# Layer 2 of a four-layer graph network: exponentials formed as [column, row], with sums from a column of ones

## Chip, cores and metric

The kernel runs on one core of one Trainium2 chip. The metric is device time in microseconds (us) of one execution. The kernel before takes 1063.96 us, the median of three runs (1063.92 to 1064.11).

## What is computed

Four graph layers are applied in turn to x, 32 batches of 512 nodes with 128 features, all float32, over one adjacency matrix of 512 x 512. Each layer normalizes x per node, clips it at zero, runs its graph part and adds the result to x. Layer 2, the one that the change is named for, is a graph attention:

```python
def _L2_gnn_ref(h, adj, W, a, bias):
    Wh = jnp.einsum('bnf,fo->bno', h, W)
    f1 = Wh @ a[:F_out, 0]
    f2 = Wh @ a[F_out:, 0]
    e = jax.nn.leaky_relu(f1[:, :, None] + f2[:, None, :], negative_slope=0.2)
    e = jnp.where(adj[None, :, :] > 0, e, -9e15)
    attention = jax.nn.softmax(e, axis=2)
    h_prime = jnp.einsum('bij,bjo->bio', attention, Wh) + bias
    return jax.nn.elu(h_prime)
...
h = jnp.maximum(_layernorm(x, axis=-1), 0.0)
x = x + _L2_gnn_ref(h, adj, L2_gnn_W, L2_gnn_a, L2_gnn_bias)
```

Layer 0 is an attention whose scores pair neighbouring nodes; layer 1 is an attention weighted by the adjacency, followed by a normalization, an aggregation over neighbours and a small two-layer network; layer 3 multiplies by one fixed attention matrix that doesn't depend on x.

## The kernel before, in words

**Tiles.** A batch is a tile of 128 partitions x 4 chunks x 128 features (C = 4 chunks of nodes, 512 elements a partition). x of all batches stays on chip in xs. A score matrix of 512 x 512 is handled as four tiles y of 128 x 512.

**Engines.** TensorE (PE) does the products, all in float32, and the transposes, as products with an identity; a float32 product of 128 x 128 stands in the trace as two passes, a transpose as one. VectorE (DVE) and ScalarE (ACT) work on the results, GpSimd (POOL) on tiles outside PSUM, SyncE loads and stores. PSUM is used as 8 tiles ("banks") of 128 x 512.

**Layer 2 before.** preln gives the normalized, transposed hT (four transposes, line 419). project_scored (line 593) multiplies hT by w2_ext of 130 columns, so that h holds the 128 features and the two scores f1 (column P) and f2 (column P + 1). attend then works with rows of the score matrix on the partitions: four transposes repeat f2 over the partitions (prow, line 419); for each of four row blocks a fused DVE operation adds the mask and takes the row's maximum (line 620); two small operations make the negative maximum nmax (lines 631 and 635); ACT applies the leaky slope (line 645) and the exponential with its row sum (line 653), both in place in y; four transposes turn each y so that columns lie on the partitions (pt, line 419); the turned block is copied out of PSUM (line 412's helper for DVE, line 410's for ACT, two blocks each; in layer 1 it is multiplied by the adjacency on DVE instead, line 662); and sixteen products with h give po (line 673). Line 950 inverts the sums, line 953 applies them, POOL adds the bias (line 954), ACT and DVE form the elu (lines 958 and 959), and POOL adds it to xs (line 960).

**Other lines that the change touches.** In layer 0, DVE forms hs and hs2, h scaled by two factors per node (lines 803 and 804); ACT rounds hs2 (line 817), POOL forms the remainder (line 818), and products use both (lines 835 and 840). In layer 1, DVE takes mean and variance of zn (lines 509 and 511), and POOL raises the variance to the power -1/2 (lines 521 and 523). Before the layers, prepare and prepare_last make masks and weights: bias (0 or NEG by the adjacency) by rows, biasT by columns for the first 256 rows.

**The order of the work.** No loop sets it. Every operation is recorded with an engine, an assumed length, what it reads and writes, and for some a port count; Plan.run then places them by its own clock, engine by engine, taking the operation that can begin first and, among those within SLACK of it, the one with the earliest turn. A turn is the start of the chain (one layer of one batch; starts are GAPS apart, a layer LAGS batches behind layer 0) plus STRETCH times the way within it. The preparation has turns of its own (PREPARED, FILLED). The port count makes the plan keep marked DVE and POOL operations apart in time. A tile's buffer comes from a room of fixed size (8 banks, 8 for scores, 6 for h). Where the plan sees PE idle for over PAUSE it puts in transposes that compute nothing (line 332, "idle"). The result is a fixed order on each engine's queue; a queue runs strictly in that order, and an instruction whose inputs are late holds up all behind it.

Of the kernel before, what the change touches and what calls it, by code (L numbers as in the profile page):

```python
# [28 lines left out]
F32 = mybir.dt.float32  # L29
# [8 lines left out]
P = 128  # L38
NEG = -9.0e15
# [18 lines left out]
SLACK = 0.05  # L58

STRETCH = 3.7  # L60

PREPARED, FILLED = (27.0, 1.0), (135.0, 1.3)

RAMP = 3.7
# [3 lines left out]
GAPS, LAGS = (5.3, 12.0, 6.7, 5.4), (0, 6, 12, 16)  # L68
# [41 lines left out]
class Plan:  # L110
# [45 lines left out]
    def run(self):  # L156
# [17 lines left out]
        for _ in range(len(self.ops)):  # L174
# [35 lines left out]
            if op.engine is PE and begin - idle[PE] > PAUSE:  # L210
                wanted = sum(s.tile is None and s.room is self.banks for s in op.slots)
                if sum(free <= idle[PE] for free in self.banks.free) > wanted:
                    self.idle_products(begin - idle[PE])
# [42 lines left out]
def kernel(  # L256
# [40 lines left out]
    sm = ctx.enter_context(tc.tile_pool(name="sm", bufs=8))  # L297

# [7 lines left out]
    def small(name, shape=(P, C)):  # L306
        return sm.tile(list(shape), F32, name=name, tag=name)
# [65 lines left out]
    biasT = const("biasT", (P, C, N2))  # L373
# [26 lines left out]
    v_offT, v_adiag, v_adiag_rep = Value(), Value(), Value()  # L400
# [50 lines left out]
    for ib in range(C):  # L451
# [6 lines left out]
            wide(e.t).bitcast(BF16)[:, 0:N], bias[:, ib, :], 0.0, None, ALU.is_gt), [v_adj[ib]], [e])  # L458
# [24 lines left out]
    def mask_first():  # L483
        for jb in range(C):
            nc.vector.tensor_scalar(biasT[:, jb, :], adjT[:, jb, 0:N2], 0.0, NEG, ALU.is_le, ALU.mult)

    op(DVE, 0.8, mask_first, v_adjT[0:H], [v_biasT])
# [7 lines left out]
    op(DVE, 0.8, mask_second, [*v_adjT[H:], v_cnt], [v_mask2T])  # L495
# [20 lines left out]
    def inv_dev(mv):  # L516
        rstd = Value()

        def emit():
            ve = small("ve")  # L520
            nc.gpsimd.tensor_scalar(ve, mv.own[:, :, 1], LN_EPS, 1.0, ALU.add, ALU.mult)
            rstd.own = small("rstd")
            nc.gpsimd.tensor_tensor(rstd.own, ve, mhalf, ALU.pow)  # L523

        op(POOL, 1.3, emit, [mv], [rstd])
        return rstd
# [81 lines left out]
    def attend(h, src, v_src, v_h, weights, v_weights):  # L608
# [32 lines left out]
        for ib in range(C):  # L641
# [18 lines left out]
            if weights is not None:  # L660
                pT = value(turned, "pT")
                op(DVE, 0.6, lambda ib=ib, pt=pt, pT=pT: nc.vector.tensor_mul(pT.t, pt.t, weights[:, :, blk(ib)]),  # L662
                   [pt, *v_weights], [pT])
            elif ib < H:
                pT = value(by_act, "pT")
                copy_op(ACT, 0.49, lambda pT=pT: pT.t, lambda pt=pt: pt.t, [pt], [pT])
            else:
                pT = value(turned, "pT")
                copy_op(DVE, 0.6, lambda pT=pT: pT.t, lambda pt=pt: pt.t, [pt], [pT])
# [15 lines left out]
    def layer0(b):  # L685
        hT, _ = preln(b, POOL)
# [30 lines left out]
        for hf in range(H):  # L717

            def emit_max(hf=hf):
# [3 lines left out]
                for k in range(2):  # L723
                    jb = 2 * hf + k
                    nc.vector.tensor_tensor_reduce(
                        wide(y[hf].t)[:, k * N2 : k * N2 + N2], node[:, hf, :], biasT[:, jb, :], 1.0, LOWEST,
# [75 lines left out]
        dve(0.08, emit_rs2, [rs, e2], [rs2], port=1)  # L802
        op(DVE, 0.6, lambda: nc.vector.tensor_mul(hs.t, h[0].t[:, :, 0:P], per_chunk(rs.own)), [rs, *h], [hs], port=1)
        op(DVE, 0.6, lambda: nc.vector.tensor_mul(hs2.t, h[0].t[:, :, 0:P], per_chunk(rs2.own)), [rs2, *h], [hs2], port=1)
# [54 lines left out]
    def layer1(b):  # L859
# [61 lines left out]
        rz = inv_dev(variances(lambda c: zn.t[:, c, :], [zn]))  # L921
# [17 lines left out]

    def layer2(b):  # L940
        hT, _ = preln(b, POOL)
        h = project_scored(hT, w2_ext, [v_w2])
        po, ssum = attend(h, lambda: h[0].t[:, :, P], h, h, None, None)
        v1 = value(by_dve, "v1")

        rs = Value()

        def emit_rs():
            rs.own = small("rs")
            nc.vector.reciprocal(rs.own, ssum[0].own)  # L950

        dve(0.1, emit_rs, ssum, [rs])
        dve(0.6, lambda: nc.vector.tensor_mul(v1.t, po[0].t, per_chunk(rs.own)), [*po, rs], [v1])  # L953
# [39 lines left out]
    def prepare():  # L993
# [24 lines left out]
        for ib in range(C):  # L1018
            dve(0.31, lambda ib=ib: nc.vector.tensor_scalar(
                bias[:, ib, :], bias[:, ib, :], 0.0, NEG, ALU.is_le, ALU.mult), [], [v_adj[ib], v_bias])  # L1020
# [5 lines left out]
        def centred(dst, src, reads, writes):  # L1026
            def emit():
                s = small("row_sum", (P, 1))
                nc.vector.tensor_reduce(s, src(), AX.X, ALU.add)
                nc.vector.tensor_scalar(s, s, 1.0 / P, None, ALU.mult)  # L1030
                nc.vector.tensor_scalar(dst(), src(), s, None, ALU.subtract)

            dve(0.5, emit, reads, writes)
# [26 lines left out]
        dve(0.35, eye, [v_eps], [eye_e])  # L1060
        for jb in range(C):
            op(POOL, 0.6, lambda jb=jb: nc.gpsimd.tensor_copy(adjTe[:, jb, :], adjT[:, jb, :]), v_adjT, [v_adjTe], port=1)
            dve(0.2, lambda jb=jb: nc.vector.tensor_add(
                adjTe[:, jb, blk(jb)], adjTe[:, jb, blk(jb)], eye_e.t[:, 0, :]), [eye_e], [v_adjTe])
# [4 lines left out]
    def prepare_last():  # L1069
# [34 lines left out]
        for kb in range(C):  # L1104
            dve(0.31, lambda kb=kb: nc.vector.tensor_scalar(
                maskT_t(kb), adjT[:, kb, :], 0.0, None, ALU.is_gt), v_adjT, [maskT[kb]])
# [37 lines left out]
        dve(0.4, emit_before, [v_n], [v_before])  # L1144
# [12 lines left out]
        dve(0.4, emit_lo, [pb, v_n], [v_lo])  # L1157
# [18 lines left out]
        for ib in range(C):  # L1176
# [9 lines left out]
            dve(0.78, emit_in, [rank_k, v_lo], [ge_lo, in_row[ib]])  # L1186
# [9 lines left out]
        dve(0.3, emit_terms, [v_e], [v_terms])  # L1196
# [53 lines left out]
        for ib in range(C):  # L1250
# [45 lines left out]
            dve(0.31, emit_last, [v_e, v_lo, num[ib]], [share[ib]])  # L1296
# [5 lines left out]
            dve(0.72, emit_diag, [], [share[ib], dg, v_diag[ib]])  # L1302
# [56 lines left out]
```

## Time and profile before

| what | value |
|---|---|
| median of the runs shown | 1063.96 us |
| the profiled execution's own time | 1063.48 us |
| its span, first to last instruction | 1061.6 us |
| TensorE clock granted | 1.000 |
| idle transposes (line 332) | 158, busy 21.7 us |
| line 673, products of attention and h in layers 1 and 2 | 2048 passes, busy 242.2 us |
| line 419, transposes of y, layers 1 and 2 | 1024, busy 130.9 us |
| line 653, exponentials of layers 1 and 2 | 256, 714 ns each, and 256 reads of the sum, 191 ns each |
| line 412, turned blocks copied by DVE | 64, 684 ns each |
| line 410, turned blocks copied by ACT | 64, 587 ns each |

A "busy" time counts the time in which at least one instruction of the group ran; consecutive instructions overlap, so the distance between their starts is shorter than one's duration. A table by stretches of the span gives, for each engine, the busy time in the stretch and the number of instructions that began in it. The table of waits names the instruction that waited, what released it, the total wait, how often, and the longest.

### The profile page before, as it was taken

The page shows a single profiled execution, that of the slowest core. Times are in us where ns is not written, and L with a number is a line of the kernel's source. Part 1 is how long each engine was busy: PE and PEld are TensorE (multiplying, and loading weights), DVE is VectorE, ACT ScalarE, POOL GpSimd, SP SyncE. Part 2 cuts the span into 40 slices and gives each one's busy share as a digit, 9 for nine tenths or more (in the row PEclk, how much of TensorE's full clock was granted, in tenths as well). Part 3 has the DMA queues.
Part 4 walks back from the last instruction along what each step waited for, and adds up shares of the span by engine and source line. Part 5 has one row for each costly group of instructions (what it writes and reads, how often), then busy time and mean ns, then how long its engine had stood idle before and what let it go on. Part 6 is the DMA issues. An engine that isn't in the chain of part 4 may idle for free.

```text
span 1061.6 us, 25176 instructions
## 1 busy us (share of the span) xinstructions
PE 1043.7 (98%) x8483; PEld 964.5 (91%) x8483; DVE 875.3 (82%) x3698; ACT 766.2 (72%) x1984; POOL 795.8 (75%) x1176
## 2 busy tenths in 40 slices
PE   8999999999999999999999999999999999999998
PEld 7888888989998999999999999999899999999997
DVE  6999999989988878888888888888888877766752
ACT  3667888789777777777877777787777777767751
POOL 6999657779787768787778778777877666576772
PEclk9999999999999999999999999999999999999999
DMA  5500000000010000000000000000000000000001
GB/s 152 126 1 12 1 12 12 2 12 12 1 32 2 21 21 22 21 21 11 2 12 11 11 12 12 11 2 12 11 12 11 12 11 11 11 22 11 21 24 37
DMA packets 56911, 20.48 MB, mean 19 GB/s; under 512 B 21584, under 2 KB 56272, under 8 KB 56784
## 3 DMA queue, kind: packets, MB, share of 16 engines
q1 hardware_dynamic: 56784, 18.90, 7.2%
q8 instruction: 67, 1.10, 0.4%
q14 instruction: 60, 0.49, 0.2%
HBM read 10.43 MB, written 8.39 MB: 18 GB/s over the span
## 4 chain that ended last, share of the span: by engine, by line
PE 86%; DVE 8%; POOL 2%; ACT 2%; issue 1%; SPq 1%; DMA 0%; DVEq 0%; POOLq 0%; ACTq 0%
PE po L673 20%; PE pt L419 16%; PE po L982 10%; PE pg L909 10%; PE proj L593 7%; PE po L835 4%; PE prow L419 3%; PE p L579 3%; PE po L978 3%; PE px L579 3%; PE pz L579 2%; PE po L840 2%; DVE st L509 1%; PE po L845 1%; PE po L832 1%
## 5 line engine op out<-in xcount | busy, mean ns | idle before, releaser
L673 PE MATMUL po<-h,pT 128*128 128x128 f32 x2048 | 242.2, 275 | 0.1
L673 PEld LDWEIGHTS po<-h,pT 128*128 128x128 f32 x2048 | 236.1, 192 | 4.7 <-issue 3.3
L558 POOL TENSOR_SCALAR xn<-xs,shift,rstd 128x128 f32<-128x128 f32 x512 | 229.3, 462 | 2.4 <-DVE top L631 0.9
L653 ACT ACTIVATE y<-y,nmax 128x512 f32<-128x512 f32 x256 | 181.7, 714 | 5.4 <-DVE nmax L635 3.9
L523 POOL TENSOR_TENSOR rstd<-ve,mhalf 128x4 f32<-128x4 f32 x160 | 171.9, 1075 | 13.3
L620 DVE CUSTOM_DVE_ANT_0 y<-prow,bias 128x512 f32<-128x512 f32 x256 | 162.5, 683 | 1.9 <-PE prow L419 1.9
L982 PE MATMUL po<-h,offT 128*128 128x128 f32 x1024 | 135.4, 275 | 0.0
L419 PE MATMUL pt<-ident,y 128*128 128x128 f32 x1024 | 130.9, 274 | 0.5 <-ACT y L653 0.3
L909 PE MATMUL pg<-adjTe,hg 128*128 128x512 f32 x256 | 130.8, 593 | 0.0
L419 PEld LDWEIGHTS pt<-ident,y 128*128 128x128 f32 x1024 | 114.9, 141 | 13.0 <-issue 7.7
L982 PEld LDWEIGHTS po<-h,offT 128*128 128x128 f32 x1024 | 124.6, 192 | 0.0
L509 DVE BATCH_NORM_STATS2 st<-xs 128x6 f32<-128x128 f32 x512 | 109.5, 274 | 7.1 <-POOL xs L960 4.5
L593 PEld LDWEIGHTS proj<-w_ext,hT 128*128 128x128 f32 x768 | 96.7, 191 | 19.1 <-issue 10.3
L593 PE MATMUL proj<-w_ext,hT 128*128 128x130 f32 x768 | 103.4, 276 | 0.7 <-ACT hT L568 0.5
L645 ACT ACTIVATE y<-y,src 128x512 f32<-128x512 f32 x128 | 84.6, 713 | 23.1 <-DVE rmax L620 23.0
L960 POOL TENSOR_TENSOR xs<-xs,em 128x512 f32<-128x512 f32 x32 | 42.0, 1313 | 77.1 <-DVE em L959 64.0
L954 POOL TENSOR_TENSOR v<-v,rows 128x512 f32<-128x512 f32 x32 | 40.9, 1279 | 72.6 <-DVE v L953 72.6
L645 ACT ACTIVATE y<-y,h 128x512 f32<-128x512 f32 x128 | 84.8, 714 | 8.1 <-DVE rmax L620 7.7
L568 ACT ACTIVATE hT<-pt 128x512 f32<-128x512 f32 x128 | 73.7, 588 | 23.4 <-PE pt L419 11.7
L662 DVE TENSOR_TENSOR pT<-pt,adjT 128x512 f32<-128x512 f32 x128 | 82.5, 679 | 5.0 <-PE pt L419 4.9
L419 PE MATMUL pt<-ident,xn 128*128 128x128 f32 x512 | 80.1, 275 | 2.4 <-POOL xn L558 1.5
L410 ACT COPY h<-proj 128x260 f32<-128x260 f32 x192 | 66.1, 371 | 12.6 <-PE proj L593 11.2
(199 smaller groups left out, 2290.9 us busy)
## 6 DMA issues: line engine op xcount, KB each, us to landing
xs<-in_x_dram SPq DMA_DIRECT2D x32, 256.0 KB, 4.0
out_dram<-yo SPq DMA_DIRECT2D x32, 256.0 KB, 2.3
u<-h SPq DMA_DIRECT2D x128, 0.5 KB, 1.8
bias<-in_adj_dram SPq DMA_DIRECT2D x4, 256.0 KB, 3.8
wts<-in_L_gnn_W_dram SPq DMA_DIRECT2D x3, 64.0 KB, 3.0
rows<-in_L_gnn_bias_dram SPq DMA_DIRECT2D x2, 64.0 KB, 3.8
wt_o<-L_gnn_others_weight_dram SPq DMA_DIRECT2D x1, 64.0 KB, 2.4
wts<-n_L_gnn_self_weight_dram SPq DMA_DIRECT2D x1, 64.0 KB, 4.0
```

The lines of the kernel that those rows point to most:

```text
L419: nc.tensor.transpose(dst(k), src(k), ident)
L509: nc.vector.bn_stats(st[:, c, :], src(c))
L523: nc.gpsimd.tensor_tensor(rstd.own, ve, mhalf, ALU.pow)
L558: nc.gpsimd.tensor_scalar(xn.t[:, c, :], src[:, c, :], shift.own[:, c : c + 1], rstd.own[:, c : c + 1], ALU.add, ALU.mult,)
L579: nc.tensor.matmul(pt.t[:, c, :], lhsT=column(hT, c), rhs=w, start=True, stop=True)
L593: nc.tensor.matmul(p[:, c, :], lhsT=column(hT, 2 * k + c), rhs=w_ext, start=True, stop=True)
L620: nc.vector.tensor_tensor_reduce(wide(y[ib].t), wide(prow.t), bias[:, ib, :], 1.0, LOWEST, ALU.add, ALU.max, rmax.own[:, ib : ib + 1],)
L645: nc.scalar.activation(yw, yw, AF.Prelu, alpha=0.2, bias=src()[:, ib : ib + 1])
L653: nc.scalar.activation(yw, yw, AF.Exp, bias=nmax.own[:, ib : ib + 1], accum_out=ssum[0].own[:, ib : ib + 1])
L673: nc.tensor.matmul(po[ib].t[:, ib, :], lhsT=pT.t[:, jb, :], rhs=h[0].t[:, jb, 0:P], start=(jb == 0), stop=(jb == C - 1),)
L909: nc.tensor.matmul(wide(pg.t), lhsT=hg.t[:, nb, :], rhs=adjTe[:, nb, :], start=(nb == 0), stop=(nb == C - 1))
L982: nc.tensor.matmul(po[ib].t[:, ib, :], lhsT=offT[:, jb, blk(ib)], rhs=h1.t[:, jb, :], start=False, stop=(jb == C - 1),)
```

## The change

Layer 2 no longer calls attend. The row maxima are found as before, with the added scores written to a tile junk that nothing reads. The scores are then formed with columns on the partitions: f1 is repeated by four transposes (p_src), nmax by four more (p_max, copied to r_max by ACT); for each of four column blocks DVE adds p_src, the column's f2 and the mask biasT, ACT applies the leaky slope, POOL (two blocks) or DVE (two blocks) adds r_max, ACT takes the exponential. The result is used by PE as it is. The score column of h is overwritten with ones by POOL, so that products of 129 columns give the row sums as column 128; they now need two banks. biasT grows to all 512 rows and becomes bfloat16, and NEG becomes a power of two.

Besides, hs2 of layer 0 is formed by ACT; layer 1's second variance comes from four squares with sums on ACT; four centred weights are formed by ACT; adjTe is copied by ACT instead of POOL; some small tiles get 14 buffers instead of 8; and the plan's constants and several port counts and lengths change.

```diff
-NEG = -9.0e15
+NEG = -(2.0**53)
-SLACK = 0.05
-STRETCH = 3.7
-PREPARED, FILLED = (27.0, 1.0), (135.0, 1.3)
-RAMP = 3.7
+SLACK = 0.10
+STRETCH = 3.3
+PREPARED, FILLED = (33.0, 1.0), (152.0, 1.7)
+RAMP = 2.9
-GAPS, LAGS = (5.3, 12.0, 6.7, 5.4), (0, 6, 12, 16)
+GAPS, LAGS = (5.1, 11.7, 6.5, 5.2), (0, 5, 11, 15)
...
-    biasT = const("biasT", (P, C, N2))
+    biasT = const("biasT", (P, C, N), BF16)
...
+    def squares(src, reads):
+        sq = Value()
+        def emit():
+            sq.own = small("sq")
+            for c in range(C):
+                nc.scalar.activation(sq_out, src(c), AF.Square, accum_out=sq.own[:, c : c + 1])
+        op(ACT, 1.55, emit, reads, [sq])
+        return sq
...
+        def emit_hs2():
+            for c in range(C):
+                nc.scalar.mul(hs2.t[:, c, :], h[0].t[:, c, 0:P], rs2.own[:, c : c + 1])
-        op(DVE, 0.6, lambda: nc.vector.tensor_mul(hs2.t, h[0].t[:, :, 0:P], per_chunk(rs2.own)), [rs2, *h], [hs2], port=1)
+        op(ACT, 1.17, emit_hs2, [rs2, *h], [hs2])
...
-        rz = inv_dev(variances(lambda c: zn.t[:, c, :], [zn]))
+        rz = inv_dev(squares(lambda c: zn.t[:, c, :], [zn]), lambda sq: sq.own, 1.0 / P)
...
     def layer2(b):
-        po, ssum = attend(h, lambda: h[0].t[:, :, P], h, h, None, None)
+        prow = repeated(lambda k: h[0].t[:, k, P + 1 : P2], h)
+        junk = parts(scores, "junk", C)
...
+            op(DVE, 0.61, emit_top, [prow, v_bias], [junk[ib], top[ib]])
...
+        p_src = repeated(lambda k: h[0].t[:, k, P : P + 1], h)
+        p_max = repeated(lambda k: nmax.own[:, k : k + 1], [nmax])
+        r_max = value(by_act, "r_max")
+        copy_op(ACT, 0.49, lambda: wide(r_max.t), lambda: wide(p_max.t), [p_max], [r_max])
+        y = [value(scores, "y") for _ in range(C)]
+        for jb in range(C):
+            op(DVE, 0.61, lambda jb=jb: nc.vector.scalar_tensor_tensor(
+                wide(y[jb].t), wide(p_src.t), h[0].t[:, jb, P + 1 : P2], biasT[:, jb, :], ALU.add, ALU.add),
+               [p_src, v_biasT, v_biasT2, *h], [y[jb]])
+            op(ACT, 0.61, lambda jb=jb: nc.scalar.activation(wide(y[jb].t), wide(y[jb].t), AF.Prelu, alpha=0.2), [], [y[jb]])
+            engine, length, on = ((POOL, 1.25, nc.gpsimd), (DVE, 0.6, nc.vector))[jb % 2]
+            op(engine, length, lambda jb=jb, on=on: on.tensor_add(
+                wide(y[jb].t), wide(y[jb].t), wide(r_max.t)), [r_max], [y[jb]], port=1)
+            op(ACT, 0.61, lambda jb=jb: nc.scalar.activation(wide(y[jb].t), wide(y[jb].t), AF.Exp), [], [y[jb]])
+        ones = Value(h[0].slot)
+        op(POOL, 0.15, lambda: nc.gpsimd.memset(h[0].t[:, :, P : P + 1], 1.0), [neg, p_src], [*h, ones])
...
+                    nc.tensor.matmul(
+                        sums(ib // 2)[:, ib % 2, 0 : P + 1], lhsT=y[jb].t[:, ib, :], rhs=h[0].t[:, jb, 0 : P + 1],
+                        start=(jb == 0), stop=(jb == C - 1),
+                    )
+            op(PE, 0.9, emit_po, [*y, ones], [po[ib // 2]])
...
+                nc.vector.reciprocal(rs[0].own[:, 2 * k : 2 * k + 2], sums(k)[:, :, P])
+            dve(0.1, emit_rs, [po[k], *rs[0:k]], [rs[k]])
+            dve(0.35, lambda k=k: nc.vector.tensor_mul(
+                v1.t[:, 2 * k : 2 * k + 2, :], sums(k)[:, :, 0:P],
...
-            op(POOL, 0.6, lambda jb=jb: nc.gpsimd.tensor_copy(adjTe[:, jb, :], adjT[:, jb, :]), v_adjT, [v_adjTe], port=1)
+            op(ACT, 0.59, lambda jb=jb: nc.scalar.copy(adjTe[:, jb, :], adjT[:, jb, :]), v_adjT, [v_adjTe])
```

## The prediction

> **What bounds the kernel now.** I read the page's busy shares first, then the chain that ended last, then the table by stretches, and last the PE timeline of one batch. The page:
>
> ```profile
> span 1061.6 us, 25176 instructions
> ...
> PE 1043.7 (98%) x8483; PEld 964.5 (91%) x8483; DVE 875.3 (82%) x3698; ACT 766.2 (72%) x1984; POOL 795.8 (75%) x1176
> ...
> PE 86%; DVE 8%; POOL 2%; ACT 2%; issue 1%; SPq 1%; DMA 0%; DVEq 0%; POOLq 0%; ACTq 0%
> ```
>
> PE is busy nearly all the span and is 86% of the chain. A busy share can hide a slow start, so the stretches decide (columns: length, then busy time of PE, its weight loads, DVE, ACT and POOL with the number of instructions, granted clock, DMA share, GB/s):
>
> ```profile
> 25.00:50.00 25.00, 23.46 (x187) 20.49 (x186) 24.07 (x148) 15.28 (x53) 23.99 (x42) 1.00 0.54 131
> ...
> 75.00:100.00 25.00, 22.37 (x181) 20.44 (x180) 24.05 (x97) 17.67 (x50) 23.89 (x35) 1.00 0.07 13
> ...
> 200.00:300.00 100.00, 100.00 (x808) 91.89 (x807) 93.20 (x407) 84.01 (x226) 79.95 (x117) 1.00 0.03 7
> ...
> 400.00:500.00 100.00, 100.00 (x823) 93.05 (x822) 85.12 (x379) 74.72 (x199) 79.18 (x117) 1.00 0.08 18
> 500.00:600.00 100.00, 100.00 (x823) 93.01 (x823) 82.29 (x353) 72.90 (x190) 79.22 (x118) 1.00 0.05 12
> 600.00:700.00 100.00, 99.95 (x827) 93.27 (x826) 83.31 (x350) 73.80 (x196) 75.86 (x112) 1.00 0.04 10
> 700.00:800.00 100.00, 100.00 (x830) 93.49 (x829) 85.94 (x347) 76.82 (x193) 77.68 (x114) 1.00 0.04 10
> ```
>
> From 150 us on PE doesn't stop, at full clock. From 25 to 100 us DVE and POOL are both 96% busy and PE falls behind: the start is theirs. From 200 to 300 us DVE at 93% and ACT at 84% still leave PE full. These two rows are my scale for how much the other engines can bear.
>
> The timeline of PE gives the rate (start, length, instruction, number):
>
> ```profile
> 501.15 1.91 PE L419 MATMUL pt<-ident,y 128*128 128x128 f32 x16
> 502.90 0.60 PE L419 MATMUL pt<-ident,zn 128*128 128x128 f32 x4
> ...
> 510.49 0.60 PE L419 MATMUL prow<-ident,h 128*128 128x128 f32 x4
> 510.92 1.06 PE L579 MATMUL px<-wts,zT 128*128 128x128 f32 x8
> ...
> 532.29 1.91 PE L419 MATMUL pt<-ident,y 128*128 128x128 f32 x16
> ```
>
> Sixteen transposes of y take 502.90 - 501.15 = 1.75 us from start to start, four repeats of a row 0.43: 0.109 us each, both kinds alike. The same group returns after 532.29 - 501.15 = 31.14 us, the period of a batch with all four layers.
>
> **PE's part of the change.** Per batch 16 transposes of y go (line 419 as called from attend), and 8 come, for p_src and p_max: 8 x 0.109 = 0.87 us less, 27.9 us over 32 batches. The 32 passes of po stay, with 129 columns for 128. Eight passes of 130 columns take 0.90 us from start to start (line 593 at 523.40), eight of 128 take 0.89 (line 673 at 518.50): 0 to 0.04 us a batch, 0 to 1.3 in all; I take 0.6. Nothing hides these terms where PE is full, and layer 2 begins only after some 200 us. The listing of the changed program's PE queue holds 167 idle transposes for 158: 35 fewer in the start, 44 more later. 9 x 0.109 is +1.0 us. The new period is 31.14 - 0.87 = 30.27 us, if nothing else takes over.
>
> **DVE.** Added per batch: four score additions (nearest row: line 967, also a PSUM tile with an SBUF one, 0.58 from start to start; fused additions of line 620, 0.61) 4 x 0.61; two additions of r_max 2 x 0.61 (line 959, 0.61); one more reciprocal 0.08; the two halves of line 953 for one, 2 x 0.34 (line 853) - 0.61. Removed: two copies of pT 2 x 0.61, hs2 0.60, the variance of zn 1.06 (515.36 to 516.42). Net +0.93 us. A bfloat16 mask beside a float32 tile is in no row; 0.58 and 0.79 (line 1264, two scalars) bound each score addition, so the net lies between +0.8 and +1.7. The four stretches shown from 400 us average 84.2%, 26.2 us a batch; 27.1 of 30.27 is 90%.
>
> **ACT.** Added: four squares with sums, each 0.32 (line 925, busy over count) and a read of the sum 0.19, 2.04; hs2 4 x 0.32; r_max 0.56. Removed: two copies 1.12, four reads of sums 0.76. Net +2.0; down to +1.3 if the exponentials and slopes without a scalar operand run as line 904 does (630 ns for 714). 74.6% of 31.14 is 23.2 us; 25.2 of 30.27 is 83%, below the 84% seen beside a full PE.
>
> **POOL.** Added: two additions of 128x512, 1.28 each (lines 917 and 960), and the memset of ones, 0.10 to 0.25 (the constants' memsets, line 521). +2.7 us. 78.0% of 31.14 is 24.3 us; 27.0 of 30.27 is 89%. It is the largest growth, on a queue that now spends 6.9 us a batch waiting:
>
> ```profile
> POOL v L954 <- DVE v L953: 72.6, 24, 10.3
> POOL xs L960 <- DVE em L959: 64.0, 26, 6.9
> ```
>
> **The waits that are added.** PE's transposes of nmax wait for DVE. Behind them stand layer 0's products; ahead, between p_src and p_max, the changed queue has some 6 to 8 us of PE work in two neighbouring batches, against 4 x 0.61 + 0.2 = 2.6 us of DVE work. Between p_max and the products that need y lie about 100 passes, 11 us, against r_max 0.56, two POOL additions 2.6 and two exponentials 1.4, some 5 us with the handovers. So PE's margin is 3.5 to 6 us, which the queues of the others can use up. POOL's additions wait for ACT; behind them stand xn of other batches, and behind xn PE's next transposes. All four y now live until the last product, and junk takes a fifth buffer of 8. I price all this at +2 us, bounds 0 and +15.
>
> **The shared reads of DVE and POOL.** A row: POOL's addition of line 855 runs from 508.20 for 0.73 us, and DVE's ltn (line 752, two SBUF inputs of 4 elements) starts at 508.23 and takes 0.71, where its median is 0.216. It waited for POOL. Another: hs (line 803, two SBUF inputs) starts at 526.89 inside a rstd of POOL (526.13 to 527.15) and takes its usual 0.68; the power reads little and holds little. So the sum that must not overlap is POOL without five rstd, 27.0 - 5.1 = 21.9, and DVE's five large operations with two SBUF inputs, 3.05, and some 17 small ones at 0.1: 26.7 of 30.27 us, 88%. It fits.
>
> The Trainium skill, page "SBUF — State Buffer", section "Who interferes with whom", speaks against this change: a DVE instruction with two SBUF inputs and a GpSimd instruction that reads SBUF exclude each other for a whole instruction. Taken for rstd too, that would make 27.0 + 4.75 = 31.8 us a batch, more than 31.14, and a kernel slower by about 20 us; the row of hs inside rstd speaks for the smaller sum.
>
> **Start and end.** From 25 to 150 us the trace has 10 hs2 (6 us), four centred weights (line 1030 and its neighbours, some 3 us) and one variance on DVE that go to ACT, and 2.5 us of copies on POOL (line 1062) that do; 4 x 0.29 (line 485) come. DVE is relieved by some 9 us, POOL by less; I take -3 us, bounds -9 and +3. The last 60 us have PE waits of some 6 us in all, taken as they are.
>
> **Sum.** 1061.6 - 27.9 + 0.6 + 1.0 + 2 - 3 = 1034.3 us of span; outside it lie 1063.48 - 1061.6 = 1.9 us. That is 1036 us, against 1063.48 for the same execution; the median is 0.5 us above that. A difference of about 0.2%, 2 us, is the least that a measurement of this kernel can tell.
>
> **Rivals.**
> *A, PE stays the bound (0.62):* 1036, its own range 1026 to 1046.
> *B, the gain is half lost (0.17):* DVE at 90% or POOL at 89% holds PE up in stretches, as both do at 96% before 100 us, where PE gets 92%. For it: both now run above their mean of 400 to 800 us; against: the 93% of 200 to 300 us. Half of 27.9 gives 1050; 1046 to 1061.
> *C, POOL's waits stay (0.14), slower:* of the 6.9 us a batch that POOL waits at the head of its queue, those for v and em are dependences and not slack. If over 4.1 us stay (31.14 - 27.0), POOL's period passes the old one. With 4.9 kept it is 31.9, 0.8 x 32 = 25 us: 1088; with all of them 33.9, some 1150. Against it: the order of the queue was made anew, and a wait at the head shrinks when the queue fills.
> *D, no effect (0.03):* the end is set elsewhere than by PE's work, so 1064. The full rows speak against it.
> *E, the start shrinks too (0.04):* all of the 9 us that DVE loses there, and no new waits: 1020 to 1026.
>
> **Numbers.** Faster: A, B and E, 0.83; same 0.03; slower 0.14. The range 1020 to 1060 takes in E, A, nearly all of B, some 0.81; C and D stay out.
>
> **What would show it.** In the changed profile: 512 transposes of y for 1024 and 384 + 128 repeats for 256; the period of layers 0 to 3 near 30.3 us; PE still at 99 to 100 in the stretches from 200 to 800, with DVE near 90, ACT near 83 and POOL near 89. B would show as PE at 95 to 98 there, with waits of PE's weight loads on POOL's or ACT's y. C would show as PE at 90 and long waits of POOL's additions on ACT. I am wrong if the products of 129 columns over two banks run slower than 0.112 us a pass, or if an instruction on y takes over a fifth longer than its nearest row.

## The result, and the profile after

| | before | after |
|---|---|---|
| median of 4 runs | 1063.94 us (1063.11 to 1064.11) | 1075.97 us (1073.15 to 1077.79) |
| ratio | | 1.0113, 95% interval 1.01 to 1.0126 |
| profiled execution | 1063.48 us, span 1061.6 | 1077.17 us, span 1075.2 |

The change makes the kernel 12 us slower; 1036 us were forecast. The page of the changed kernel, in the same order as that of the kernel before (span; busy time, share and instructions of each engine; the chain that ended last):

```profile
span 1075.2 us, 24867 instructions
...
PE 1032.6 (96%) x8236; PEld 936.8 (87%) x8236; DVE 960.4 (89%) x3594; ACT 813.1 (76%) x2224; POOL 885.9 (82%) x1268
...
DVE 41%; PE 35%; POOL 11%; ACT 6%; issue 3%; SPq 2%; DMA 1%; DVEq 0%; POOLq 0%; ACTq 0%
```

PE has 11 us less to be busy with and the span is 13.6 us longer. The chain, which went through PE for 86% of its length, now goes through DVE for 41% and POOL for 11%. DVE has grown by 85 us, POOL by 90, ACT by 47. The stretches of the changed kernel (length, then PE, its weight loads, DVE, ACT, POOL, the granted clock, DMA share, GB/s):

```profile
200.00:300.00 100.00, 95.64 (x729) 83.63 (x728) 92.76 (x362) 89.99 (x255) 80.63 (x116) 1.00 0.03 7
...
400.00:500.00 100.00, 96.53 (x780) 87.90 (x779) 92.52 (x331) 78.35 (x214) 79.32 (x116) 1.00 0.07 17
500.00:600.00 100.00, 98.73 (x805) 90.72 (x804) 93.76 (x353) 78.30 (x215) 88.46 (x125) 1.00 0.06 12
600.00:700.00 100.00, 98.71 (x807) 91.02 (x806) 94.43 (x349) 77.25 (x217) 88.29 (x127) 1.00 0.05 12
700.00:800.00 100.00, 98.75 (x792) 89.73 (x791) 95.22 (x364) 80.06 (x221) 88.23 (x130) 1.00 0.04 10
```

PE is at 95.6 to 98.8% where it was full, and from 400 us on it starts 780 to 807 passes in 100 us where it started 823 to 830. A busy share hides short waits, since consecutive passes overlap. So I took from each trace the distances between the starts of consecutive passes: for each kind of pass, the distance at the lowest quarter is its work, and what goes beyond it by more than 15 ns is waiting. Summed over the span:

| us | work of PE | waits of PE | DVE busy | of it above the groups' medians | POOL busy |
|---|---|---|---|---|---|
| before | 1018.9 | 37.1 | 875.3 | 18.1 | 795.8 |
| after | 993.0 | 73.3 | 960.4 | 69.8 | 885.9 |

**PE's work fell by 25.9 us, as forecast (-26.3). Its waits grew by 36.2.** (The span grew by 3.3 us more than these two give; distances under the 15 ns and the two ends are not counted in them. Other ways of sorting the passes into kinds give 23 to 27 us for the first and 34 to 38 for the second.) They are spread: 0 to 200 us 21.6 (25.2 before), 200 to 400 us 16.0 (3.7), 400 to 800 us 16.6 (3.9), the rest 19.0 (4.3). The column "above the medians" is the part by which DVE's instructions last longer than the median of their own group, so it is time without added work. A group here is a line's instructions of one shape that also wait for and raise the same semaphores, and what is under some 50 ns isn't counted. With groups by line and shape alone the two numbers are 28 and 77: the growth is nearly the same, 49 us for 51.7.

The groups of DVE in the changed kernel that show it (busy us and mean ns of one, then the idle time before), and the one of ve in the kernel before:

```profile
L994 DVE SCALAR_TENSOR_TENSOR y<-prow,h,biasT 128x512 f32<-128x512 f32 x128 | 89.0, 743 | 0.0
...
L999 DVE TENSOR_TENSOR y<-y,r_max 128x512 f32<-128x512 f32 x64 | 62.7, 1003 | 4.7 <-ACT r_max L415 4.2
...
L897 DVE TENSOR_TENSOR ve<-q,mv 128x4 f32<-128x4 f32 x32 | 12.4, 387 | 0.0
```

```profile
L881 DVE TENSOR_TENSOR ve<-q,mv 128x4 f32<-128x4 f32 x32 | 5.1, 158 | 0.0
```

The score addition of line 994 takes 743 ns each time, 60 more than the fused additions. The additions of r_max (line 999) take 1003 ns in the mean; the table of that line gives the least, the median and the longest:

```profile
L999 DVE TENSOR_TENSOR y<-y,r_max x64: 656/692/3715, 195.3 to 1040.2; 128x512 f32<-128x512 f32 x64
```

The small ve, unchanged, took 158 ns in the mean (line 881 of before) and now takes 387, while its median went only from 154 to 158: some of the 32 wait long. What holds them is seen in one stretch. DVE's timeline of the changed kernel:

```profile
624.94 2.35 DVE L999 TENSOR_TENSOR y<-y,r_max 128x512 f32<-128x512 f32 x2
...
628.89 1.19 DVE L722 SCALAR_TENSOR_TENSOR ls<-sc 128x4 f32<-128x4 f32 x1
```

and POOL's in the same stretch:

```profile
624.87 1.28 POOL L1040 TENSOR_TENSOR xs<-xs,em 128x512 f32<-128x512 f32 x1 [2.02 <-DVE ve L897]
...
627.55 2.51 POOL L999 TENSOR_TENSOR y<-y,r_max 128x512 f32<-128x512 f32 x2
```

DVE's two additions start 0.07 us after POOL's addition and take 2.35 us; two of them take some 1.2 without it, so they wait till POOL ends at 626.15. The ls of four elements starts inside POOL's additions of y and ends at 630.08, when they have ended (630.06): 1.19 us for some 0.2. These waits count as busy time. They are the rule and not two chosen cases: of the DVE instructions with two SBUF inputs, 85 start while POOL is in an operation of over 0.6 us that reads SBUF (its power rstd apart, and with over 0.4 us of it to go), and 83 of these take over 100 ns more than usual, half of the 85 some 750 ns or more. In the kernel before there are 28 such meetings, and 21 take longer. POOL's rstd does not hold DVE: 140 such instructions start inside one in the changed kernel, and none takes over 34 ns more.

The table of waits of the changed kernel (total us, times, longest):

```profile
ACT y L1001 <- POOL y L999: 22.2, 27, 2.7
...
PEld pt L424 <- ACT y L672: 18.3, 48, 1.8
POOL y L999 <- ACT r_max L415: 17.6, 12, 2.2
...
PEld proj L612 <- ACT hT L587: 10.6, 13, 2.4
```

The chain r_max, addition, exponential has waits of its own (22.2 and 17.6 us). But PE's weight loads wait on other layers too: on layer 1's y (line 672 is in attend) for 18.3 us, where the wait for y of layers 1 and 2 together took 2.6 in the kernel before, and on hT of any layer (line 587) for 10.6, before 5.1. Loads overlap the products, so not all of this is lost to PE; but PE itself has 9.1 us idle before line 612's products and 1.8 before layer 2's (line 1014). What was lost is not lost at layer 2's products.

### The profile page after: what moved, and what is told of

Its sections match the earlier page's. It is cut to its first block, busy times and chain, and to the rows that moved or that the text cites. A ratio compares the mean times of both kernels' runs of the same rounds, so it can differ in the third digit from the quotient of the medians.

```text
span 1075.2 us, 24867 instructions
## 1 busy us (share of the span) xinstructions
PE 1032.6 (96%) x8236; PEld 936.8 (87%) x8236; DVE 960.4 (89%) x3594; ACT 813.1 (76%) x2224; POOL 885.9 (82%) x1268
## 4 chain that ended last, share of the span: by engine, by line
DVE 41%; PE 35%; POOL 11%; ACT 6%; issue 3%; SPq 2%; DMA 1%; DVEq 0%; POOLq 0%; ACTq 0%
PE po L1062 6%; DVE st L514 5%; DVE y L994 5%; DVE junk L970 5%; DVE pT L680 4%; PE po L685 4%; PE po L851 4%; PE pt L424 4%; DVE y L639 3%; PE pg L925 3%; PE proj L612 3%; PE prow L424 3%; POOL y L999 2%; POOL xn L577 2%; PE po L1014 2%
## 5 line engine op out<-in xcount | busy, mean ns | idle before, releaser
L1014 PE MATMUL po<-h,y 128*128 128x129 f32 x1024 | 126.7, 275 | 1.8 <-ACT y L1001 1.8
L1014 PEld LDWEIGHTS po<-h,y 128*128 128x128 f32 x1024 | 120.3, 191 | 2.8 <-ACT y L1001 2.1
L685 PE MATMUL po<-h,pT 128*128 128x128 f32 x1024 | 121.4, 276 | 1.0 <-DVE pT L680 1.0
L514 DVE BATCH_NORM_STATS2 st<-xs 128x6 f32<-128x128 f32 x512 | 109.8, 277 | 13.6 <-POOL xs L1040 10.8
L685 PEld LDWEIGHTS po<-h,pT 128*128 128x128 f32 x1024 | 117.4, 192 | 2.1 <-DVE pT L680 1.8
L612 PEld LDWEIGHTS proj<-w_ext,hT 128*128 128x128 f32 x768 | 94.7, 191 | 15.5 <-ACT hT L587 10.6
L1001 ACT ACTIVATE y<-y 128x512 f32<-128x512 f32 x128 | 78.0, 629 | 36.3 <-POOL y L999 22.2
L999 POOL TENSOR_TENSOR y<-y,r_max 128x512 f32<-128x512 f32 x64 | 88.6, 1400 | 17.7 <-ACT r_max L415 17.6
L672 ACT ACTIVATE y<-y,nmax 128x512 f32<-128x512 f32 x128 | 90.8, 713 | 9.0 <-DVE nmax L654 2.7
L997 ACT ACTIVATE y<-y 128x512 f32<-128x512 f32 x128 | 78.6, 628 | 18.1 <-DVE y L994 13.5
L970 DVE CUSTOM_DVE_ANT_0 junk<-prow,bias 128x512 f32<-128x512 f32 x128 | 87.8, 686 | 2.2
L994 DVE SCALAR_TENSOR_TENSOR y<-prow,h,biasT 128x512 f32<-128x512 f32 x128 | 89.0, 743 | 0.0
L424 PEld LDWEIGHTS pt<-ident,xn 128*128 128x128 f32 x512 | 61.8, 141 | 26.2 <-POOL xn L577 13.9
```

Source lines behind the costliest of these rows:

```text
L424: nc.tensor.transpose(dst(k), src(k), ident)
L514: nc.vector.bn_stats(st[:, c, :], src(c))
L612: nc.tensor.matmul(p[:, c, :], lhsT=column(hT, 2 * k + c), rhs=w_ext, start=True, stop=True)
L685: nc.tensor.matmul(po[ib].t[:, ib, :], lhsT=pT.t[:, jb, :], rhs=h[0].t[:, jb, 0:P], start=(jb == 0), stop=(jb == C - 1),)
L970: nc.vector.tensor_tensor_reduce(wide(junk[ib].t), wide(prow.t), bias[:, ib, :], 1.0, LOWEST, ALU.add, ALU.max, rmax.own[:, ib : ib + 1],)
L994: op(DVE, 0.61, lambda jb=jb: nc.vector.scalar_tensor_tensor(wide(y[jb].t), wide(p_src.t), h[0].t[:, jb, P + 1 : P2], biasT[:, jb, :], ALU ...
```

## The experiments

The expectations name four theories of where the time went. At first theory 1 was that DVE binds, with what it waits for POOL's reads; theory 2, that the plan's new constants made a worse order; theory 3, that the chain over the transposed maximum binds; theory 4, that the steps moved to ACT lengthen other chains. Theory 1 was later split: 1a, DVE's load; 1b, POOL's load and its reads. Ratios are against the kernel before, with their 95% intervals. "Waits" are PE's waits as in the table above.

### The parts, undone one by one

The change has three parts: layer 2's new form (**L**), the steps moved to ACT with the new preparation, the changed port counts and deeper small buffers (**M**), and the plan's constants (**C**; without M, in e6 and e8, the deeper buffers come with them). The constants are

```diff
-SLACK = 0.05
+SLACK = 0.10
-STRETCH = 3.7
+STRETCH = 3.3
-PREPARED, FILLED = (27.0, 1.0), (135.0, 1.3)
+PREPARED, FILLED = (33.0, 1.0), (152.0, 1.7)
-RAMP = 3.7
+RAMP = 2.9
-GAPS, LAGS = (5.3, 12.0, 6.7, 5.4), (0, 6, 12, 16)
+GAPS, LAGS = (5.1, 11.7, 6.5, 5.2), (0, 5, 11, 15)
```

e3, the changed kernel with the constants of before (the diff above turned round):

> The change with the plan's constants of before (slack, stretch, preparation's turns, ramp, gaps, lags); the operations are those of the change. Theory 1: the operations set the time, so within 8 us of 1076. Theory 2: 1036 to 1055. Theory 3: within 8 us of 1076.

e4, the changed kernel with layer2 and attend of before:

```diff
-        prow = repeated(lambda k: h[0].t[:, k, P + 1 : P2], h)
...
+        po, ssum = attend(h, lambda: h[0].t[:, :, P], h, h, None, None)
```

> The change with layer 2 as before (attend with transposes); the rest of the change stays: squares and hs2 on ScalarE, the preparation, the plan's constants. Theory 1: VectorE is 1.6 us a batch lighter than before, TensorE is full at the old period of 31.1 us, and the start is shorter: 1050 to 1064. Theory 2: the constants cost the time here as well, 1070 to 1085. Theory 3: 1050 to 1064.

e5, the kernel before with layer 2's new form alone:

```diff
-        po, ssum = attend(h, lambda: h[0].t[:, :, P], h, h, None, None)
+        prow = repeated(lambda k: h[0].t[:, k, P + 1 : P2], h)
...
-    biasT = const("biasT", (P, C, N2))
+    biasT = const("biasT", (P, C, N), BF16)
```

> The kernel before with layer 2's new form alone (with the bfloat16 mask by columns that it needs); work of layers 0 and 1, the preparation and the plan's constants as before. Theory 1 (VectorE and its waits for GpSimd's reads set the time; the moves to ScalarE relieve it): VectorE carries 1.7 us a batch more than in the change, so slower than the change, 1085 to 1120. Theory 4 (the moves to ScalarE of layers 0 and 1 lengthen the chains that TensorE waits for, layer 2's new form gains): 1035 to 1060.

e6, e5 with the new constants and

```diff
+    sm_norm = ctx.enter_context(tc.tile_pool(name="sm_norm", bufs=14))
```

> Layer 2's new form with the change's plan constants and its deeper buffers of small tiles, without the moves to ScalarE, the changed preparation and the changed port counts. Theory 1: 1075 to 1100, VectorE at 95% and more. Theory 4: 1035 to 1055.

e7, e4 with the constants of before (so part M alone):

> Layer 2 and the plan's constants as before; only the moves to ScalarE (hs2, squares, preparation), the port counts and the deeper small buffers of the change. Theory 1: VectorE is relieved, 1050 to 1064. Theory 4: 1072 to 1090, as with the change's constants (1077.6). Theory 2 (the constants): 1055 to 1064, since they are those of before.

e8, the kernel before with the new constants and sm_norm:

> The kernel before with the change's plan constants alone, and the deeper small buffers that they need. Theory 1 and theory 4: within 6 us of 1064. Theory 2: 1072 to 1090, the constants spread the work so that TensorE waits.

| parts | run | us | ratio (95%) | waits | DVE busy | POOL busy |
|---|---|---|---|---|---|---|
| none | before | 1063.9 | 1 | 37.1 | 875.3 | 795.8 |
| M | e7 | 1065.49 | 1.0014 (1.0005 to 1.0024) | 39.7 | 846.2 | 788.7 |
| C | e8 | 1088.8 | 1.0231 (1.0216 to 1.0247) | 63.9 | 899.9 | 797.1 |
| M, C | e4 | 1077.59 | 1.0132 (1.0117 to 1.0147) | 51.4 | 853.1 | 790.6 |
| L | e5 | 1129.66 | 1.0614 (1.0589 to 1.0638) | 118.5 | 996.5 | 910.5 |
| L, C | e6 | 1110.8 | 1.044 (1.0425 to 1.0456) | 107.7 | 1020.7 | 895.5 |
| L, M | e3 | 1103.37 | 1.0372 (1.035 to 1.0395) | 93.6 | 959.6 | 899.3 |
| L, M, C | after | 1075.97 | 1.0113 (1.01 to 1.0126) | 73.3 | 960.4 | 885.9 |

Layer 2's new form costs 66 us alone, 22 beside C, 38 beside M and nothing (-1.6) beside both, although it takes work from PE in each of them. M gives back 26 to 35 us where L is there, 11 beside C and nothing by itself. C gives back 19 to 27 with L, and costs 12 to 25 without it. So theory 4 falls (e7: no loss), and theory 2 holds only half: with L the new constants are the better ones. Many of the expected ranges were missed: e3, e5 and e6 came out above all of theirs, and e7 between two. The stretch from 400 to 800 us of e5, in one row:

```profile
400.00:800.00 400.00, 378.07 (x2988) 343.53 (x2987) 366.49 (x1415) 268.80 (x674) 337.43 (x471) 0.98 0.05 11
```

PE at 94.5%, DVE at 92 and POOL at 84.

### DVE's part

e1: DVE's two additions read the maximum in PSUM, not its copy in SBUF, so that they don't compete with POOL's reads:

```diff
+            if engine is POOL:
...
+                    wide(y[jb].t), wide(y[jb].t), wide(p_max.t)), [p_max], [y[jb]])
```

> The change, except that VectorE's two additions of the row maximum read it from PSUM (p_max) and not from its copy in SBUF, so that they have one SBUF input. Theory 1 (VectorE is the bound, and a good part of its time is waiting for GpSimd's reads of SBUF): the two additions fall from a mean of 1003 ns to about 690 ns, VectorE's busy time falls by 20 us or more, and the time from 1076 to 1050 to 1066 us. Theory 2 (the plan's new constants and order cost the time): 1072 to 1080. Theory 3 (the chain through the transposed maximum is too long for TensorE's queue): 1070 to 1080, since the chain is as long as before.

1075.83 us, 1.0109 (1.0093 to 1.0124): a miss for theory 1, within the ranges of the others. DVE's time above the medians fell from 69.8 to 51.2 us, yet PE's waits are 71.9. Its order is not that of the changed kernel, since these two additions no longer have a port count and read another tile. In the stretch from 200 to 300 us PE falls to 90.5% (last section), but that is not the whole of it: from 400 to 800 us, at full clock, e1 begins 3191 passes and the changed kernel 3175, so the lighter DVE brought next to nothing there either.

e2: no additions of the maximum:

```diff
-            op(engine, length, lambda jb=jb, on=on: on.tensor_add(
-                wide(y[jb].t), wide(y[jb].t), wide(r_max.t)), [r_max], [y[jb]], port=1)
```

> The change without the four additions of the row maximum (the maximum is found, repeated and copied, but not subtracted, so the exponentials are those of the unshifted scores). TensorE's work is that of the change. Theory 1: VectorE loses 63 us of busy time for its two additions and much of the 30 us of waits of its small operations; GpSimd loses 89 us; TensorE is the bound again, the period is near the 30.3 us that was forecast, and the time 1036 to 1050. Theory 2: over 1065. Theory 3: the exponentials no longer need the maximum, but TensorE still waits for it before its transposes (6.5 us of idle time), so 1060 to 1070.

1053.6 us, 0.99 (0.9884 to 0.9917), between the expected ranges; waits 60.6; DVE busy 891.7, POOL 779.2. Some 10 us are gained on the kernel before, yet most of the added waits are still there: the additions are not the whole cause.

e9: layer 2 subtracts one common shift per batch as the bias of the exponential, so that row maxima, nmax's transposes and the additions go:

```diff
-                nc.vector.tensor_tensor_reduce(
...
+            nc.vector.tensor_reduce(tops[0].own, wide(prow.t), AX.X, ALU.max)
...
+                wide(y[jb].t), wide(y[jb].t), AF.Exp, bias=nmax.own), [nmax], [y[jb]])
```

> The change with one shift for a whole batch in layer 2 in place of a maximum for each row: two maxima over repeated rows of scores (an upper bound of every score of the batch), given to the exponential as its bias; the four masked maxima, the transposes and the copy of the row maxima and the four additions go. It leaves out rows without an edge and rows whose scores all lie some 87 below the batch's largest. Theory 1 (VectorE's and GpSimd's load in layer 2, with their waits for each other, is what the new form costs): VectorE and GpSimd each lose over 80 us of busy time, TensorE 14 us of work, TensorE's waits fall from 73 us to below 45: 1020 to 1040. If the order of the plan alone is at fault: above 1050.

1046.76 us, 0.9832 (0.9816 to 0.9848), slightly missed; waits 62.5 though DVE is at 853.4 and POOL at 785.7 us. It has no chain over a transposed maximum, and most of the waits are there all the same: theory 3 isn't the main cause. e10 is e9 with the constants of before:

> The kernel with one shift for a whole batch in layer 2 (leaves out what that one leaves out), with the plan's constants of before. Theory 1: the light layer 2 runs as well with either constants, 1015 to 1045. If the constants matter by themselves, as in the kernel before, where the new ones cost 25 us, this is faster than the same kernel with the new ones; if they are good for the new layer 2, as in the change, where the old ones cost 27 us, it is slower by 15 us and more.

1039.25 us, 0.9759 (0.9742 to 0.9777), within theory 1's range, but 7.5 us faster than e9, so the constants matter here too; waits 42.7. The mean row of its stretches from 400 to 800 us:

```profile
sum 400.00, PE 400.00 PEld 370.79 DVE 342.81 ACT 326.12 POOL 319.96; mean PE 100.00 PEld 92.70 DVE 85.70 ACT 81.53 POOL 79.99
```

With DVE and POOL at 86 and 80%, near the 84 and 78 of before, PE is full again and 25 us come out, of some 35 by which PE's work is below that of the kernel before. It is the fastest version here; it leaves out what e9's expectation names.

### Who adds the maximum

e11: all four additions on POOL; e12: all four on DVE, from PSUM, without r_max:

```diff
-            engine, length, on = ((POOL, 1.25, nc.gpsimd), (DVE, 0.6, nc.vector))[jb % 2]
+            engine, length, on = POOL, 1.25, nc.gpsimd
```

```diff
-        copy_op(ACT, 0.49, lambda: wide(r_max.t), lambda: wide(p_max.t), [p_max], [r_max])
...
+            op(DVE, 0.6, lambda jb=jb: nc.vector.tensor_add(
+                wide(y[jb].t), wide(y[jb].t), wide(p_max.t)), [p_max], [y[jb]])
```

> The change with all four additions of the row maximum on GpSimd. VectorE loses its two (63 us busy, of which some 20 waiting), GpSimd gains 82 us. Theory 1a (VectorE's load is what binds): 1050 to 1068. Theory 1b (GpSimd's load and its reads are what binds): 1085 to 1115.

> The change with all four additions on VectorE, reading the maximum from PSUM, without the copy in SBUF. VectorE has 4 x 0.61 us a batch in place of 2 x 1.0, some 15 us more in all, GpSimd loses 89 us and ScalarE 18 us; the additions no longer meet GpSimd's reads. Theory 1a: 1080 to 1105. Theory 1b: 1050 to 1068.

e11: 1131.77 us, 1.0642 (1.0597 to 1.0687), above both ranges; waits 125.5; DVE busy 954.7, only 6 us less than in the changed kernel where 63 were expected, and 85.2 above the medians. e12: 1060.94 us, 0.9965 (0.9952 to 0.9978), waits 57.5; DVE busy 956.1, 30.5 above the medians. The mean rows from 400 to 800 us, of e11:

```profile
sum 400.00, PE 373.30 PEld 335.47 DVE 355.58 ACT 291.40 POOL 338.28; mean PE 93.33 PEld 83.87 DVE 88.90 ACT 72.85 POOL 84.57
```

and of e12:

```profile
sum 400.00, PE 398.63 PEld 364.47 DVE 373.71 ACT 317.58 POOL 310.00; mean PE 99.66 PEld 91.12 DVE 93.43 ACT 79.39 POOL 77.50
```

With DVE at 93% PE is at 99.7% in e12; with DVE at 94% it is at 98.2% in the changed kernel (means of the four stretches). So DVE's busy share doesn't bind by itself, which speaks against 1a, and the additions on POOL become the suspects. But e12's waits (57.5) are still 20 us above those of the kernel before, and both runs have orders of their own.

### POOL's time, its reads, or the chain

e13 and e14 put POOL's work back into e12, for nothing: three memsets of a spare buffer, or two additions of constants.

```diff
+        pad = value(by_act, "r_max")
+        for _ in range(2):
+            op(POOL, 0.97, lambda: nc.gpsimd.memset(wide(pad.t).bitcast(BF16), 0.0), [p_max], [pad])
+        op(POOL, 0.56, lambda: nc.gpsimd.memset(wide(pad.t), 0.0), [p_max], [pad])
```

```diff
+            op(POOL, 1.25, lambda k=k: nc.gpsimd.tensor_add(
+                wide(pad.t), bias[:, k, :], bias[:, k + 2, :]), [p_max, v_bias], [pad], port=1)
```

> The version with all four additions on VectorE from PSUM (1060.9 us), and in each batch three memsets on GpSimd of a buffer that nobody reads, 2.5 us in all, about as long as the two additions that GpSimd did in the changed kernel. They read nothing and nobody waits for what they write; only GpSimd's time is taken. If the loss comes from GpSimd's time (its queue too full), this is back at 1072 to 1080 us. If it comes from the reads of SBUF that shut VectorE out, or from the chain that waits for the additions, it stays at 1058 to 1066.

> The same, with two GpSimd additions of 128x512 of two constants from SBUF in place of the memsets (2 x 1.28 us): GpSimd's time and its reads, but nobody waits for what they write. If the reads that shut VectorE out make the loss, this is at 1070 to 1080 us and the memsets are not; VectorE's time over its medians rises by 15 us or more against the memsets. If the loss is in the chain (the exponentials wait for GpSimd's additions), both stay at 1058 to 1066. If it is GpSimd's time, both are at 1072 to 1080.

e13: 1071.9 us, 1.0077 (1.006 to 1.0093), waits 69.7. e14: 1076.59 us, 1.0114 (1.0099 to 1.0129), waits 72.7. Most of the loss is back without a chain to layer 2's exponentials (the spare buffer is shared, so its next user does wait, 21.9 us of ACT in e14), and DVE's time above the medians is 13.7 us higher with reads than without (44.7 and 31.0; with groups by line and shape alone 62 and 34). But both also have another order than e12, so the step isn't proven. e16, e17 and e18 keep the plan's lengths and cut only what POOL really does. In each pair the traces have the same instructions in the same order on DVE, ACT and POOL, and on PE, but for one record that is missing in e18:

```diff
-            op(POOL, 0.97, lambda: nc.gpsimd.memset(wide(pad.t).bitcast(BF16), 0.0), [p_max], [pad])
+            op(POOL, 0.97, lambda: nc.gpsimd.memset(wide(pad.t)[:, 0:4], 0.0), [p_max], [pad])
```

```diff
-                wide(pad.t), bias[:, k, :], bias[:, k + 2, :]), [p_max, v_bias], [pad], port=1)
+                wide(pad.t)[:, 0:4], bias[:, k, 0:4], bias[:, k + 2, 0:4]), [p_max, v_bias], [pad], port=1)
```

```diff
+            some = slice(0, 4 if engine is POOL else N)
...
+                wide(y[jb].t)[:, some], wide(y[jb].t)[:, some], wide(r_max.t)[:, some]), [r_max], [y[jb]], port=1)
```

> The kernel with three idle memsets a batch on GpSimd (1071.9 us), its memsets cut to 4 elements each. The plan still counts 2.5 us for them, so PE, VectorE and ScalarE run the same instructions in the same order; only GpSimd's real time is 2.2 us a batch less. If GpSimd's time made the 11 us that the memsets cost, this is at 1058 to 1064 us. If the order that the plan made around them did, it stays at 1068 to 1073.

> The kernel with two idle GpSimd additions a batch (1076.6 us), cut to 4 of 512 elements. The order of the instructions of PE, VectorE and ScalarE stays what it was; GpSimd's time and its reads go. If time and reads made the 16 us, this is at 1056 to 1064 us; if the order did, it stays at 1072 to 1077.

> The changed kernel (1076.0 us), where GpSimd's two additions in each batch cover 4 of the 512 columns (the maximum isn't subtracted from the rest). Plan, order and waits stay what they are; GpSimd loses 2.3 us a batch of time and reads, and the chain to the exponentials grows 1.2 us shorter. If GpSimd's additions make the loss, PE's saved 26 us come out and this is at 1045 to 1062 us. If the order that the plan made does, it stays at 1070 to 1076.

| pair in one order | full work | cut | difference | POOL busy | DVE above medians | waits |
|---|---|---|---|---|---|---|
| idle memsets, e13 and e16 | 1071.9 | 1065.82 | 6.1 us | 852.7, 784.9 | 31.0, 35.1 | 69.7, 63.2 |
| idle additions, e14 and e17 | 1076.59 | 1053.26 | 23.3 us | 870.2, 798.0 | 44.7, 21.2 | 72.7, 53.3 |
| layer 2's additions, after and e18 | 1075.97 | 1068.73 | 7.2 us | 885.9, 812.6 | 69.8, 59.3 | 73.3, 66.9 |

Ratios of the cut ones: e16 1.002 (1.0011 to 1.0029), e17 0.9901 (0.9886 to 0.9916), e18 1.0041 (1.003 to 1.0052). e16 fell between its two expectations, e17 went beyond the lower one. In its order, some 70 us of POOL's time cost 6 us where it reads nothing; in another, 23 where it reads SBUF, and DVE's time above the medians grows by 23.5 with it (29 by line and shape alone). That the reads alone make 23 out of 6 isn't shown, since the orders of e13 and e14 differ: in the changed kernel's own order POOL's two additions read SBUF too and cost 7, and e18 still waits 66.9. Neither of e18's expectations was met. The rest lies with the order and with what else the queues hold in it.

e15, e12 with the constants of before:

> The version with all four additions on VectorE from PSUM, with the plan's constants of the kernel before. The common shift gained 7.5 us by these constants, the changed kernel lost 27. If the constants of before fit every kernel that PE bounds, this is at 1045 to 1055 us. If the new ones fit whatever carries layer 2's additions, it is slower than 1061, up to 1085.

1070.01 us, 1.0059 (1.0044 to 1.0074), against 1060.94 for e12: the new constants are better by 9 us here. e17 keeps layer 2's row maxima whole and is, at 1053.26 us, faster than both kernels: it is e12 with two tiny idle operations a batch that only change what the plan lays around them. e16 is e12 with three such, and takes 1065.82: next to the same work, three orders, 12.6 us apart.

## Why the prediction was wrong, point by point

- **PE's part: right.** Transposes of y are 512 for 1024; work fell 25.9 us for 26.3. A pass of 129 columns takes 275 ns in the mean, as one of 128 did, and consecutive ones start 112 ns apart in the median, the price in the text.
- **ACT: right.** +46.9 us, 1.47 a batch, between +1.3 and +2.0; the exponentials and slopes without a scalar operand take 629 and 628 ns, as the nearest row said. **POOL: right in sum.** +90.1 us, 2.8 a batch for 2.7.
- **DVE: the sum was mis-sized.** +85.1 us, 2.66 a batch, for +0.93 (bounds 0.8 to 1.7). The waits inside instructions grew by 51.7 us, 1.6 a batch, which the sum didn't have; the score addition took 743 ns for 683, 7.7 us in 128 (the bound of 0.79 held it). The remaining 25.7 us, 0.8 a batch, are near what the count of instructions gave. From 400 to 800 us DVE is at 94% for the 90 of the text. The text's own alarm, an instruction on y over a fifth longer than its nearest row, went off at line 999: 1003 ns for 688, by waiting, since the median is 692.
- **The shared reads, "It fits", and the term of the added waits that went with it, +2 us: the step that failed.** The text put DVE's waits for POOL's reads at nothing, because their sum is 88% of the period, and PE's added waits at +2, or -1 together with the start. Measured: 51.7 us more inside DVE's instructions, and 36.2 us more of PE's waits. 88% is an average. It would fit if both engines could choose when to run; both run in a fixed order and meet where they meet, and then one waits for what is left of the other's instruction, as the two timelines show. Such meetings rose from 28 to 85. The row that told it was in the text (ltn, 0.71 us for 0.216), and was counted at nothing. It was no exception: 14 of the 32 ltn of the kernel before take 712 to 724 ns, and the median of 216 lies between them and the rest. The other row, hs inside rstd, was read rightly. How many of PE's 36 us come from DVE's waits is shown only in part, see "Open". The Trainium skill's page "SBUF — State Buffer", section "Who interferes with whom", was right on the exclusion (83 of the 85 meetings). The text's estimate from it, with rstd counted, was a kernel slower by about 20 us; the sign and the size came near, but not by its mechanism, since rstd holds nothing and no period of 31.8 us is seen.
- **The waits: +2 us with bounds 0 to 15; measured, with the start, 36.** The starts of yo, layer 3's result, lie 31.1 us apart from 507 to 756 us, as before and not 30.27: the waits took all that PE saves in a batch. The margins of PE around p_max (3.5 to 6 us) were worked out for layer 2's products, and there PE waits little: line 1014 has 1.8 us idle before it. It waits at layer 1's y, at hT, at nmax's transposes. A later DVE or POOL delays all that stands behind it on its queue, whatever the layer.
- **The start: right in sign.** Layer 1's first result (res, line 951, before 935) starts at 139 us for 163, but by some 300 us the lead is gone.
- **Rivals.** B named the mechanism (PE held up in stretches, at 95 to 98%, with waits of its weight loads on ACT's y) and bounded it at half the gain; it took all of it and 12 us more. C's mark, PE at 90% and long waits of POOL's additions on ACT, isn't there: 17.6 us in all, 0.55 a batch. A's condition, that PE stays the bound, did come true once DVE and POOL stayed at their old load: e10, 1039 us.
- **Left out: the order.** The text took the plan's new constants as part of a queue "made anew". They alone move the time by 8 to 27 us, in either direction (e4 and e7, e9 and e10, e12 and e15, e3 and the changed kernel).

**Open.** Of the 36 us of waits, 6.4 are shown to be POOL's two additions in that order (after and e18; 7.2 us of the time). The others can't be divided between the order itself, DVE's own larger load and its two additions with SBUF operands: every other run that changes one of these also gets another order, and orders alone differ by up to 27 us. Why the constants that suit the heavy layer 2 cost time with a lighter one (e8; e9 and e10) was not found.

## What to carry to other kernels

An operation taken from the bound is worth its time only if what replaces it fits beside it in the actual order: where the helpers stood at 82 and 75%, they grew by 85 us (52 of them waits) and 90 to save 26 on PE, and all of it was given back. Count instructions of two engines that shut each other out as waits wherever they can meet, and look at the spread (least, median, longest) of a small unchanged instruction to see the price. Where a plan sets the order, compare in one order: keep the planned lengths and shrink the real work; a comparison of two plans measures the plans too.

## What was not expected of the hardware

**A stop of PE can cost more than its length.** In e1, PE stands still from 235.5 to 238.0 us and from 239.1 to 242.2, and the granted clock drops; ten-microsecond stretches of e1 (PE's busy time is the second number, the clock is behind POOL's):

```profile
230.00:240.00 10.00, 6.63 (x58) 6.20 (x56) 9.90 (x39) 7.14 (x20) 9.57 (x18) 1.00 0.00 0
240.00:250.00 10.00, 7.65 (x41) 6.13 (x42) 9.71 (x26) 8.72 (x29) 3.52 (x6) 0.66 0.05 5
250.00:260.00 10.00, 10.00 (x75) 8.51 (x74) 8.91 (x36) 6.60 (x16) 9.32 (x11) 1.00 0.08 24
```

The clock is 0.66 in the second row and 1.00 in the third; from 270 to 280 us it is 0.83 once more, after a stop of 2.20 us. The sixteen transposes that end that stop take 3.75 us in e1's timeline, for 1.91 in the kernel before. The length of a stop alone doesn't tell it: in the changed kernel PE stands still for 2.16 us at 442 us, and the clock stays at 1.00. From 200 to 300 us e1 begins 679 passes, the changed kernel 729. Yet this is not why e1 gained nothing in the end: at 506 us its seventh yo starts, as in the changed kernel (507). In e5 and e11, with the most waits, the mean clock is 0.988 and 0.987.

**The DVE addition with a bfloat16 mask took longer than the all-float32 ones.** With a float32 tile in PSUM, a bfloat16 one in SBUF and a scalar per partition, 128x512 takes 743 ns (735 to 752 over 128 of them), against 672 (line 967) and 683 (line 620) in the mean for the all-float32 rows of before, 60 to 70 more. Which of its operands does it was not tried.
